# Scan layer of a four-layer network: state rows of 400 columns instead of 385, states starting at the seventeenth column

## The chip, the cores and the metric

The kernel runs on one core of a Trainium2 chip. Its time is the device time of one execution in microseconds (us). The core has five engines that run side by side and wait for each other on semaphores: TensorE (PE, with its weight loads as PEld), VectorE (DVE), ScalarE (ACT), GpSimd (POOL) and SyncE (SP), which here issues most of the DMAs. On-chip memory (SBUF) has 128 partitions; every engine works on all partitions at once and walks along the bytes of each. Matmuls write to a second memory, PSUM.

## The reference

An image batch x of 3 x 256 x 48 x 48 goes through four layers, each added to its own input after a group normalisation: an attention block (layer 0), a convolution whose 3x3 kernels are mixed from eight experts for each image (layer 1), a plain 3x3 convolution (layer 2), and a state-space scan (layer 3). The change touches layer 3 alone. Cut to what matters there, with b the image, t one of 2304 pixels in order, d one of 512 channels and n one of 16 states:

```python
dt = softplus(dt_raw @ dt_proj_w.T + dt_proj_b)          # (b, t, d)
def step(hst, inp):                                      # hst: (b, d, n)
    dt_t, B_t, C_t, u_t = inp
    dA = exp(dt_t[:, :, None] * A)
    hst = hst * dA + dt_t[:, :, None] * B_t[:, None, :] * u_t[:, :, None]
    y_t = einsum('bdn,bn->bd', hst, C_t)
    return hst, y_t
y = (ys + u * D) * silu(z)
out = y @ out_proj_w.T
```

So every channel and state is a recurrence h(t) = dA(t) h(t-1) + dtu(t) B(t) along the pixels, and the output sums h(t) C(t) over the 16 states. All data are float32.

## The kernel before, in words

Layers 0 to 2 fill the first 2025 us of the span. They use none of the tiles of the change.

In layer 3 the pixels of an image are cut into six chunks of CH = 384, so there are 18 chunks. A chunk's scan is 8 steps: four groups m of 128 channels, and two halves h of the 16 states. That makes 144 steps in the list `steps` (L1696). A step has one state tile `hs`: 128 partitions by 8 rows (two groups g by four q). A row is 385 float32: the state before the chunk in column 0, and one state for each of the 384 pixels behind it. A row of 385 floats is 1540 bytes, 24 times 64 and 4 more. There are three buffers for `hs`, two for `hc`, `dtr` and `dtur`, all in one pool (L1662).

A step goes through these stations:

- `first_states` (L1720): ACT copies eight starting states into column 0 (L1724), from a zero tile in the first chunk of an image, else from the states that the chunk before left.
- `fill` (L1705): the term dtu * B is written into columns 1 to 384. DVE writes the four rows with q = 0 and 1 from PSUM (L1711), POOL the four with q = 2 and 3 from the tile `dtur` (L1715).
- `decay` (L1732): ACT takes exp(dt * A) of one row into one of three PSUM slots `ps_da` (L1740). Column 0 of a slot holds 0.
- `scan` (L1745): DVE runs the recurrence over all 385 columns of one row, in place (L1748). The first column is multiplied by 0 and gets the first state added, so it passes the state on. Eight scans a step; the first four take the rows that DVE has filled, the last four those of POOL.
- `last_states` (L1726): ACT keeps the last column of the eight rows for the next chunk (L1730).
- `times_c` (L1752): POOL multiplies the eight rows by C into the tile `hc` (L1765). The very last step does this on DVE in two halves (L1759).
- `add_states` (L1770): PE folds `hc` into the sum `ps_y` (L1782), which starts with u * D (L1777), and `gate` (L1787) multiplies by silu(z) on DVE (L1789).

The order is written out by hand in the loop from L1800, and `keep_order` ties PE, DVE, ACT and POOL to it. In one step DVE issues eight scans and then the fill of the next step; POOL issues the fill of the next step and then `times_c` of this one; three decays run ahead of the scans. Between the scans the loop places the preparation of later chunks (`plan`, L1373): normalisation, projections, softplus (DVE at L1326 and L1327), and silu on ACT with two table loads (L1278, L228). A POOL fill may start when `times_c` has let go of the buffer that it writes; `times_c` of a step waits for that step's last scan; a scan of the second half waits for POOL's fill.

Of the kernel before, what the change touches and what calls it, by code (L numbers as in the profile page):

```python
# [9 lines left out]
F32 = mybir.dt.float32  # L10
I32 = mybir.dt.int32
AF = mybir.ActivationFunctionType
ALU = mybir.AluOpType
# [3 lines left out]
P = 128  # L17
# [8 lines left out]
CH = 384  # L26
# [10 lines left out]
DS = 16  # L37
DTR = 16
DCONV = 4


SUM_MIN, SUM_MAX = 1e-18, 1e18
# [41 lines left out]
def net(  # L84
# [21 lines left out]
    nc = tc.nc  # L106
# [1005 lines left out]
    def divide(block, *parts):  # L1112

        at = 0
        for name, rows, shape in parts:
            n = int(np.prod(shape))
            v = block[:rows, at : at + n]
            at += n
            if len(shape) > 1:
                names = "abc"[: len(shape)]  # L1120
                v = v.rearrange(
                    f"p ({' '.join(names)}) -> p {' '.join(names)}", **dict(zip(names, shape))
                )
            yield name, v

    def w3_rooms():
# [3 lines left out]
        w3v.update(divide(  # L1130
            block, ("w3sb", P, (NW3,)), ("wtap", P, (DCONV, CT, DI * P)), ("dtsb", DTR + 1, (DI * P,)),
            ("amat", P, (DI * DS,)), ("rep", P, (4, 32)), ("less", P, (2, P)), ("zero", P, (8,)),
            ("xn0", P, (CT, CH + DCONV - 1)), ("xn1", P, (CT, CH + DCONV - 1)),
        ))
# [23 lines left out]
    def x2_rooms():  # L1158
# [3 lines left out]
        winx, cwb = (t for _, t in divide(  # L1162
            block, ("winx", P, (CT, DI * P)), ("cwb", P, (DCONV, DI * P))
        ))
        nc.sync.dma_start(winx, w3x.rearrange("(t p) n -> p t n", p=P))
        for k in range(DCONV):
            nc.sync.dma_start(cwb[:, k, :], convw[k : k + 1, :].broadcast_to([P, DI * P]))
# [80 lines left out]
    def tokens(k):  # L1248

        xn = k.xn = room(k, "xn")  # L1250
        if k.c == 0:
            nc.gpsimd.memset(xn[:, :, : DCONV - 1], 0.0)
        else:
            nc.scalar.copy(xn[:, :, : DCONV - 1], k.before.xn[:, :, CH:])
        for ct in range(CT):
# [247 lines left out]
    with ExitStack() as l1:  # L1503
# [117 lines left out]
        for n, (k, h) in enumerate(halves):  # L1621
            layer, b = units[k]
# [33 lines left out]
    with ExitStack() as l3:  # L1656
# [5 lines left out]
        scn = l3.enter_context(tc.tile_pool(name="scn", bufs=2, reuse_waits="tile"))  # L1662
# [34 lines left out]
        tiles = {}  # L1697
# [7 lines left out]
        def fill(s):  # L1705

            at, m, h = steps[s]
            k = chunks[at]
            hs = tiles[s]
            bb = k.bc[0][:, 2 * h : 2 * h + 2, :].unsqueeze(2).broadcast_to([P, 2, 2, CH])  # L1710
            nc.vector.tensor_tensor(  # L1711
                hs[:, :, 0:2, 1:],
                k.ps[:, :, :CH].unsqueeze(1).broadcast_to([P, 2, 2, CH]), bb, ALU.mult,
            )
            nc.gpsimd.tensor_tensor(  # L1715
                hs[:, :, 2:4, 1:],
                k.rows[m][1].unsqueeze(1).broadcast_to([P, 2, 2, CH]), bb, ALU.mult,
            )

        def first_states(s):  # L1720
            at, m, h = steps[s]
            src = zero if chunks[at].c == 0 else state[m, h]
            hs = tiles[s] = scn.tile([P, 2, 4, CH + 1], F32, name="hs", bufs=3)
            nc.scalar.copy(hs[:, :, :, 0], src.rearrange("p (g q) -> p g q", g=2))  # L1724

        def last_states(s):  # L1726
            at, m, h = steps[s]
            if chunks[at].c < NCH - 1:
                t = state[m, h] = wp.tile([P, 8], F32, name=f"hst{m}{h}")
                nc.scalar.copy(t.rearrange("p (g q) -> p g q", g=2), tiles[s][:, :, :, CH])  # L1730

        def decay(n):  # L1732

# [10 lines left out]

        def scan(s, part):  # L1745
            g, q = parts_of_step[part]
            b = tiles[s][:, g, q, :]
            nc.vector.tensor_tensor_scan(  # L1748
                b, slots[(8 * s + part) % 3][:, : CH + 1], b, 0.0, ALU.mult, ALU.add
            )  # L1750

        def times_c(s):  # L1752
            at, m, h = steps[s]
            cb = chunks[at].bc[1][:, 2 * h : 2 * h + 2, :].unsqueeze(2)
            hc = scn.tile([P, 2, 4, CH], F32, name="hc")
            if s == len(steps) - 1:

                for g in range(2):
                    nc.vector.tensor_tensor(  # L1759
                        hc[:, g], tiles[s][:, g, :, 1:],  # L1760
                        cb[:, g].broadcast_to([P, 4, CH]), ALU.mult,
                    )
                tiles[s] = hc
                return
            nc.gpsimd.tensor_tensor(  # L1765
                hc, tiles[s][:, :, :, 1:], cb.broadcast_to([P, 2, 4, CH]), ALU.mult
            )
            tiles[s] = hc

# [24 lines left out]
        k.rows = {0: spread(k, 0)}  # L1794
        spread_pe(k, 0)
        first_states(0)
        fill(0)
        for n in range(3):
            decay(n)
        for s, (at, m, h) in enumerate(steps):  # L1800
            if m == 0 and h == 1 and at + 2 <= last:
                fetch(at + 2)
            for part in range(8):
                j = 4 * m + 2 * h + part // 4
                scan(s, part)
                decay(8 * s + part + 3)
                if part == 0 and h == 0:
                    c, n = (at, m + 1) if m + 1 < DI else (at + 1, 0)
                    if c <= last:
                        rows = getattr(chunks[c], "rows", {})  # L1810
                        chunks[c].rows = {**rows, n: spread(chunks[c], n)}
                if part == 4 and s + 1 < len(steps):
                    first_states(s + 1)
                if part % 4 == 1:
                    run(at, j, MID)
                if part % 4 == 2:
                    run(at, j, DONE)
                if h == 1 and part == 7 and s >= 3:
                    gate(*steps[s - 3][:2])
                if part % 4 == 3:  # L1820
                    run(at, j, LATE)
                if part == 3:
                    run(at, j, PE_)
            if s + 1 < len(steps):
                fill(s + 1)
            last_states(s)
            times_c(s)
            run(at, 4 * m + 2 * h + 1, PE_)
            if s >= 1:
# [129 lines left out]
```

## Time and profile before

| what | number |
|---|---|
| time, median of 3 runs | 3457.79 us (3455.21 to 3458.74) |
| the profiled execution's own time | 3459.61 us |
| its span, first to last instruction | 3458.2 us |
| DVE busy over the span | 2940.7 us (85%) |
| POOL busy over the span | 1430.7 us (41%) |
| ACT busy over the span | 2351.8 us (68%) |
| PE busy over the span | 3125.3 us (90%) |
| granted TensorE clock, mean | 0.944 |
| first scan to last scan | 2027.6 to 3436.0 us |

Busy shares are means over layers with different limits. A line of the profile gives line number, engine and operation, what is written from what (with partitions and elements), how often, the busy time together and the mean of one, and after the bar the idle time of the engine before it with what ended it.

### The profile page before, as it was taken

The numbers are of one execution on the slowest core, as the hardware profiler recorded it, in microseconds if no ns is written. First come the engines' busy times: TensorE is split into PE (matmuls) and PEld (weight loads), VectorE is DVE, ScalarE is ACT, GpSimd is POOL, SyncE is SP. The second block draws the span as 40 slices with busy tenths as digits, with TensorE's granted clock in tenths as the row PEclk, the third lists the DMA queues.
The fourth block names the chain that finished last, engine by engine and source line by source line (L and its number), as shares of the span: only waits on it lengthen the run. The fifth ranks groups of instructions, "written<-read, shape, count | busy, mean of one in ns | idle before, by whom it ended". The sixth has DMA issues, their size and how long they took to land.

```text
span 3458.2 us, 51943 instructions
## 1 busy us (share of the span) xinstructions
PE 3125.3 (90%) x20170; PEld 1499.8 (43%) x20170; DVE 2940.7 (85%) x3234; ACT 2351.8 (68%) x3508; POOL 1430.7 (41%) x385
## 2 busy tenths in 40 slices
PE   7999999999999999879999988888888888888885
PEld 4334343443433335447777743333343443333331
DVE  4799899859899994579965379999999999999998
ACT  3788888748888884422224457777777777777774
POOL 0000000000000001110000059999999999999997
PEclk9999999999999999989999989889999999988987
DMA  4000000010000003746402134445444444444441
GB/s 178 14 8 10 8 10 8 8 42 6 10 6 8 10 8 112 249 170 224 139 21 68 46 97 109 115 100 118 116 105 110 106 107 114 116 117 106 117 111 43
DMA packets 167603, 273.95 MB, mean 79 GB/s; under 512 B 30049, under 2 KB 134561, under 8 KB 165426
## 3 DMA queue, kind: packets, MB, share of 16 engines
q1 hardware_dynamic: 154114, 250.48, 26.9%
q10 hardware_dynamic: 13232, 20.06, 1.8%
q8 instruction: 160, 2.62, 0.3%
q14 instruction: 97, 0.79, 0.1%
HBM read 223.12 MB, written 47.10 MB: 78 GB/s over the span
## 4 chain that ended last, share of the span: by engine, by line
PE 54%; DVE 32%; ACT 8%; DMA 3%; issue 2%; POOL 0%; SPq 0%; DVEq 0%; ACTq 0%; POOLq 0%
DVE hs L1748 21%; PE ps_s L637 16%; PE acc L650 14%; PE ps_c L1513 8%; DVE hs L1711 4%; PE ps_g L1222 2%; PE ps_s L1030 2%; ACT ps_da L1740 2%; PE ps_y L461 2%; PE ps_m L664 1%; DVE u L295 1%; PE ps_m L710 1%; ACT L1278 1%; ACT L228 1%; PE acc L528 1%
## 5 line engine op out<-in xcount | busy, mean ns | idle before, releaser
L1748 DVE TENSOR_TENSOR_SCAN hs<-ps_da,hs 128x385 f32<-128x385 f32 x1152 | 1005.6, 938 | 54.4 <-ACT ps_da L1740 35.6
L641 ACT ACTIVATE pt<-ps_s 128x1024 f32<-128x1024 f32 x972 | 942.4, 1022 | 154.8 <-PE ps_s L637 142.2
L856 DVE TENSOR_TENSOR part<-part,pt 128x2048 f32<-128x2048 f32 x396 | 906.6, 2289 | 41.3 <-ACT pt L641 18.5
L1740 ACT ACTIVATE ps_da<-dtr,u 128x384 f32<-128x384 f32 x1152 | 656.0, 582 | 271.3 <-DVE hs L1748 248.4
L163 POOL TENSOR_TENSOR rstd<-ve,mhalf 128x2 f32<-128x2 f32 (+1 forms) x26 | 16.3, 629 | 1477.0 <-DVE ve L161 1477.0
L637 PE MATMUL ps_s<-q,kt 32*128 32x512 f32 (+1 forms) x4320 | 576.4, 592 | 0.1
L650 PE MATMUL acc<-pt,vt 128*32 128x512 f32 (+1 forms) x4320 | 520.9, 561 | 0.2
L1765 POOL TENSOR_TENSOR hc<-hs,x 128x3072 f32<-128x3072 f32 x72 | 446.3, 6198 | 19.8 <-DVE hs L1748 16.5
L1513 PE MATMUL ps_c<-vt,u 128*128 128x288 f32 x1728 | 433.9, 412 | 21.0 <-DVE u L262 21.0
L1765 POOL TENSOR_TENSOR hc<-hs,bc 128x3072 f32<-128x3072 f32 x71 | 438.8, 6181 | 18.6 <-DVE hs L1748 17.2
L1264 PE MATMUL ps_g<-u 128*128 128x384 f32 x1152 | 387.7, 491 | 8.2 <-ACT sz L1349 3.5
L1513 PEld LDWEIGHTS ps_c<-vt,u 128*128 128x128 f32 x1728 | 331.8, 193 | 117.8 <-issue 19.3
L1264 PEld LDWEIGHTS ps_g<-u 128*128 128x128 f32 x1152 | 214.4, 190 | 180.6 <-ACT ps_da L1740 18.7
L637 PEld LDWEIGHTS ps_s<-q,kt 32*128 32x128 f32 x4320 | 195.3, 183 | 199.1 <-issue 120.2
L1782 PE MATMUL ps_y<-hc,u 128*32 128x384 f32 x2304 | 244.8, 548 | 13.8 <-POOL hc L1765 13.8
L1715 POOL TENSOR_TENSOR hs<-dtur,x 128x1536 f32<-128x1536 f32 x72 | 248.4, 3450 | 6.9 <-DMA dtur<-dtud 6.9
L1715 POOL TENSOR_TENSOR hs<-dtur,bc 128x1536 f32<-128x1536 f32 x72 | 249.5, 3465 | 0.0
L650 PEld LDWEIGHTS acc<-pt,vt 128*32 128x32 f32 x4320 | 94.4, 108 | 353.4 <-issue 326.7
L1310 PE MATMUL ps_g<-wconv,u 17*128 17x384 f32 x144 | 79.2, 684 | 82.8 <-ACT x L1331 82.8
L1782 PEld LDWEIGHTS ps_y<-hc,u 128*32 128x32 f32 x2304 | 64.4, 117 | 172.4 <-issue 151.6
L321 POOL MEMSET xpad<- 128x212 f32 x12 | 5.6, 468 | 313.0 <-ACT xpad L1564 234.5
L1529 ACT COPY cb<-ps_c 128x288 f32<-128x288 f32 x48 | 19.2, 400 | 162.9 <-PE ps_c L1513 145.1
(246 smaller groups left out, 3685.3 us busy)
## 6 DMA issues: line engine op xcount, KB each, us to landing
wconv<-in_we SPq DMA_DIRECT2D x144, 384.0 KB, 4.3
dtr<-dtd SPq DMA_DIRECT2D x288, 192.0 KB, 3.9
dtur<-dtud SPq DMA_DIRECT2D x288, 96.0 KB, 4.2
wconv<-xd SPq DMA_DIRECT2D x36, 384.0 KB, 4.3
x<-bcd SPq DMA_DIRECT2D x72, 192.0 KB, 5.7
dtd<-x SPq DMA_DIRECT2D x36, 384.0 KB, 2.9
bc<-bcd SPq DMA_DIRECT2D x72, 192.0 KB, 6.1
yc<-ycat ACTq DMA_DIRECT2D x18, 576.0 KB, 5.0
```

The costliest lines, as they stand in the source:

```text
L637: nc.tensor.matmul(s[:, j, cols], kt[r, mt * P : (mt + 1) * P], q[r, :n], start=True, stop=True,)
L641: nc.scalar.activation(p[:, h0 : h0 + 2, :], s, AF.Exp)
L650: nc.tensor.matmul(acc[h * HD : (h + 1) * HD, :n], vt[:, mt, g * P + h * HD : g * P + (h + 1) * HD], p[:, h, cols], start=mt == 0, stop=mt ...
L856: ): nc.vector.tensor_tensor(part, first, p, ALU.add)
L1264: nc.tensor.matmul(bank[m % 2], w3v["wtap"][:, tap, ct, m * P : (m + 1) * P], k.xn[:, ct, tap : tap + CH], start=tap == 0 and ct == 0, sto ...
L1513: nc.tensor.matmul(pc[:, :HN], u[:, i, dy, ct, m * P : (m + 1) * P], vt[:, i, ct, dy * TW : dy * TW + HN], start=ct == 0 and dy == 0, stop ...
L1711: nc.vector.tensor_tensor(hs[:, :, 0:2, 1:], k.ps[:, :, :CH].unsqueeze(1).broadcast_to([P, 2, 2, CH]), bb, ALU.mult,)
L1715: nc.gpsimd.tensor_tensor(hs[:, :, 2:4, 1:], k.rows[m][1].unsqueeze(1).broadcast_to([P, 2, 2, CH]), bb, ALU.mult,)
L1740: nc.scalar.activation(slots[n % 3][:, 1 : CH + 1], chunks[at].rows[m][0][:, q, :], AF.Exp, scale=amat[:, col : col + 1],)
L1748: nc.vector.tensor_tensor_scan(b, slots[(8 * s + part) % 3][:, : CH + 1], b, 0.0, ALU.mult, ALU.add)
L1765: nc.gpsimd.tensor_tensor(hc, tiles[s][:, :, :, 1:], cb.broadcast_to([P, 2, 4, CH]), ALU.mult)
L1782: nc.tensor.matmul(k.y_ps[32 * q : 32 * q + 32, :CH], fold, hc[:, g, q, :], start=False, stop=h == 1 and g == 1,)
```

## The change

The rows of `hs` become ROW + CH = 400 columns long, 1600 bytes or 25 times 64. The first state moves from column 0 to column 15, and the 384 states from columns 1 to 384 to columns 16 to 399. A scan runs over columns 15 to 399, again 385 of them. Everything that reads or writes the tile is moved along. Sizes, counts and engines of the instructions stay.

```diff
+ROW = 16
...
             nc.vector.tensor_tensor(
-                hs[:, :, 0:2, 1:],
+                hs[:, :, 0:2, ROW:],
                 k.ps[:, :, :CH].unsqueeze(1).broadcast_to([P, 2, 2, CH]), bb, ALU.mult,
             )
             nc.gpsimd.tensor_tensor(
-                hs[:, :, 2:4, 1:],
+                hs[:, :, 2:4, ROW:],
...
-            hs = tiles[s] = scn.tile([P, 2, 4, CH + 1], F32, name="hs", bufs=3)
-            nc.scalar.copy(hs[:, :, :, 0], src.rearrange("p (g q) -> p g q", g=2))
+            hs = tiles[s] = scn.tile([P, 2, 4, ROW + CH], F32, name="hs", bufs=3)
+            nc.scalar.copy(hs[:, :, :, ROW - 1], src.rearrange("p (g q) -> p g q", g=2))
...
-                nc.scalar.copy(t.rearrange("p (g q) -> p g q", g=2), tiles[s][:, :, :, CH])
+                nc.scalar.copy(t.rearrange("p (g q) -> p g q", g=2), tiles[s][:, :, :, ROW + CH - 1])
...
-            b = tiles[s][:, g, q, :]
+            b = tiles[s][:, g, q, ROW - 1 :]
...
-                        hc[:, g], tiles[s][:, g, :, 1:],
+                        hc[:, g], tiles[s][:, g, :, ROW:],
...
-                hc, tiles[s][:, :, :, 1:], cb.broadcast_to([P, 2, 4, CH]), ALU.mult
+                hc, tiles[s][:, :, :, ROW:], cb.broadcast_to([P, 2, 4, CH]), ALU.mult
```

## The prediction

> **What bounds the kernel now.** The change touches only the scan layer, so I read first the busy time of each engine over that stretch (2025 to 3441 us; columns: length, then busy us and instructions of PE, PEld, DVE, ACT, POOL, then clock and DMA).
>
> ```profile
> core 0: us, PE busy (x) PEld busy (x) DVE busy (x) ACT busy (x) POOL busy (x), PEclk, DMA share, GB/s
> 2025.00:3441.00 1416.00, 1164.49 (x4876) 530.07 (x4874) 1358.98 (x1521) 1082.74 (x2070) 1368.86 (x289) 0.89 0.45 108
> ```
>
> DVE is busy for 1359 of 1416 us and POOL for 1369: both 96 to 97%. The page's share of POOL over the whole span (41%) hides that. Next, who waited for whom in that stretch: first DVE's and ACT's waits, then POOL's.
>
> ```profile
> ACT ps_da L1740 <- DVE hs L1748: 248.4, 399, 4.1
> ```
> ```profile
> DVE hs L1748 <- ACT ps_da L1740: 35.6, 53, 1.5
> DVE hs L1748 <- POOL hs L1715: 3.8, 1, 3.8
> ```
> ```profile
> POOL hc L1765 <- DVE hs L1748: 33.8, 31, 1.6
> POOL hs L1715 <- DMA dtur<-dtud: 6.9, 1, 6.9
> POOL hc L1765 <- PE ps_g L1222: 2.6, 2, 1.4
> POOL hc L1765 <- DVE x L1789: 1.8, 1, 1.8
> ```
>
> DVE waited for POOL once, 3.8 us, at the first step. POOL waited for DVE 31 times, ACT 399 times. So **DVE sets the pace**, and POOL is the next bound, close behind: it has 33.8 + 2.6 + 1.8 = 38.2 us of idle time in 144 steps, 0.265 us a step. The page's chain agrees: DVE 32% of the span, POOL 0%. Third, the groups that touch the tile `hs`, on the page:
>
> ```profile
> L1748 DVE TENSOR_TENSOR_SCAN hs<-ps_da,hs 128x385 f32<-128x385 f32 x1152 | 1005.6, 938 | 54.4 <-ACT ps_da L1740 35.6
> ...
> L1765 POOL TENSOR_TENSOR hc<-hs,x 128x3072 f32<-128x3072 f32 x72 | 446.3, 6198 | 19.8 <-DVE hs L1748 16.5
> ...
> L1765 POOL TENSOR_TENSOR hc<-hs,bc 128x3072 f32<-128x3072 f32 x71 | 438.8, 6181 | 18.6 <-DVE hs L1748 17.2
> ...
> L1715 POOL TENSOR_TENSOR hs<-dtur,x 128x1536 f32<-128x1536 f32 x72 | 248.4, 3450 | 6.9 <-DMA dtur<-dtud 6.9
> L1715 POOL TENSOR_TENSOR hs<-dtur,bc 128x1536 f32<-128x1536 f32 x72 | 249.5, 3465 | 0.0
> ```
>
> A step costs POOL 6.19 + 3.46 = 9.65 us. DVE's steps take 9.0 us in the middle of a chunk and 10.9 where the preparation at L1326 and L1327 falls (starts of first scans, from the timeline); the mean is 9.81. POOL falls behind in the short steps and catches up in the long ones.
>
> **The change part by part.** No instruction is added, removed or moved. The built program of the changed kernel has the same instructions in the same order with the same waits on PE, DVE, ACT, POOL and SP, DMA issues included. Element counts stay: 385 a scan, 1536 a fill, 3072 a `times_c`. So all that can change is the **duration of the accesses to `hs`**, and of those to `hc`, which lies behind `hs` in its pool: the built program puts the three `hs` buffers at 0, 32 and 0 bytes past a multiple of 64 before, and `hc` at 32; after, all of them at 0.
>
> *Scans, 1152 on DVE, on the path.* In the old tile row r starts 1540 r bytes in, which is 4r past a multiple of 64. Eight rows by two kinds of buffer give sixteen different starts, so the old trace already holds the experiment. Durations (min, median, max) of the scans, and three successive steps, which use three different buffers:
>
> ```profile
> L1748 DVE TENSOR_TENSOR_SCAN hs<-ps_da,hs x1152: 931/934/964, 2027.6 to 3436.0; 128x385 f32<-128x385 f32 x192
> ```
> ```profile
> 3394.09 6.91 DVE L1748 TENSOR_TENSOR_SCAN hs<-ps_da,hs 128x385 f32<-128x385 f32 x8
> ...
> 3403.21 6.91 DVE L1748 TENSOR_TENSOR_SCAN hs<-ps_da,hs 128x385 f32<-128x385 f32 x8
> ...
> 3411.88 6.91 DVE L1748 TENSOR_TENSOR_SCAN hs<-ps_da,hs 128x385 f32<-128x385 f32 x8
> ```
>
> Eight scans take 6.91 us whatever the buffer. Sorted scan by scan, row 0 takes 960.3 ns in a buffer at 0 and 960.1 ns in the one at 32 (the first scan of a step is the long one); row 7 of the buffer at 32 starts 60 bytes past a multiple, which is where column 15 of the new rows puts every scan, and takes 933.3 ns, against 932.6 in a buffer at 0. Starts follow each other every 850 ns in all rows. I take **0** for the scans. The ends: every scan at the lowest duration, 931, instead of the mean 938, would give 1152 x 7 ns = 8 us; every scan 0.7 ns longer (933.3 for 932.6) costs 0.8 us.
>
> *DVE's fills, 144, on the path.* By buffer they take 1740.4, 1740.2 and 1740.3 ns. I take 0; the spread of the row over a chunk's two kinds of step (1732 to 1748) bounds it at 144 x 8 ns = 1.2 us either way.
>
> *POOL's fills and `times_c`.* By `hs` buffer: 3457.5, 3457.0, 3458.4 and 6188.9, 6190.1, 6189.8 ns. No buffer shows anything, but in each at least seven of eight rows are off a multiple of 64, so a tile with all rows on one is not in the trace. The nearest rows are those above: every second chunk keeps B and C in a block called x, 32 bytes past a multiple of 64, the others in bc, at 0, and their own rows of 384 columns stay there. The aligned operand makes `times_c` 17 ns shorter and the fill 15 ns longer. I take 0 for the pair, within 32 ns a step. **Faster bound**: if POOL took no time at all, DVE would save its one wait, 3.8 us; nothing else on the path waits for POOL but the tail, where PE's last sums start at 3439.0 us, when L1777 ends, 0.3 us behind POOL's end at 3438.7. So POOL alone can't bring more than about 4 us. **Slower bound, near**: the slowest `times_c` and fill (6273 and 3523) against the medians (6197 and 3448) are 0.15 us a step, under the 0.265 of idle time, so hidden but for the last chunk, where no preparation lets POOL catch up: some ten steps x 0.15 = 1.5 us. **Slower bound, far**: the last step's products run on DVE beside POOL, and the first of them is held up:
>
> ```profile
> 3432.50 6.18 POOL L1765 TENSOR_TENSOR hc<-hs,bc 128x3072 f32<-128x3072 f32 x1
> ...
> 3437.29 4.67 DVE L1759 TENSOR_TENSOR hc<-hs,bc 128x1536 f32<-128x1536 f32 x2
> ```
>
> The two took 3.00 and 1.75 us: 1.26 us lost. Both POOL instructions of each step losing that would cost (2.51 - 0.265) x 144 = 323 us. My value lies by the near rows.
>
> *ACT's copies* (L1724 and L1730, 264 of 192 ns, steps of 400 columns instead of 385): all lie between 185 and 207 ns; 15 ns x 264 = 4 us on an engine that waits 248 us for DVE. If that cover were gone it would be those 4 us. *PE's reads of `hc`* keep their shape; median 486 ns; PE is in the chain only in the tail, with 16 such matmuls, so 0.
>
> Sum: 0 for DVE, at most 32 ns x 10 = 0.3 us in the tail from POOL. From the profiled execution that is 3459.6 us (span 3458.2 and 1.4 around it); that one lies 1.8 above the median, so against the median the forecast is **3457.8 us**, no change.
>
> *The Trainium skill against the change.* The page GPSIMD Engine Reference, section 3.1, gives two-input `tensor_tensor` about 2.5 cycles an element because both inputs share one read port, and 4497 ns for 2048 elements; addresses are no term in it. At that rate, 2.196 ns, `times_c` would be 6.75 us (an estimate from that page), and this trace has 6.19: there is no stall on top of the rate that alignment could take away, and by the page the sum is 0 too. The page SBUF — State Buffer, section "Who interferes with whom", knows one contention only, the lock on the port pair of VectorE and GpSimd. By it the first rival below costs nothing.
>
> **The rivals.**
> 1. *Slower: POOL becomes the bound.* With every row, `hs` buffer and `hc` on multiples of 64, accesses of POOL's two inputs and output, or of POOL and DVE, may fall together. It decides from 0.265 us a step on (2.7% of 9.65). A fifth of what L1759 lost on each of the two instructions is 0.50 us: (0.50 - 0.265) x 144 = 34 us, 3492. For it: POOL's 97%, and that the aligned fill is the longer one. Against it: 15 ns is all that the rows show.
> 2. *Faster: the scans get shorter.* 931 ns for all gives 8 us, 3450; it needs 6 ns a scan to pass 0.2%. Against it: sixteen starts without a difference.
> 3. *The change does only half of what it says.* Scans start at 60 past a multiple of 64, and B and C of every second chunk stay at 32. If alignment matters to POOL but only with all operands aligned, half the chunks gain. The time is then bounded as above: 3454 to 3458.
>
> **How the numbers follow.** Nothing changes: 0.70. Rival 3: 0.10. Rival 1: 0.12. Rival 2: 0.08. A measurement of this kernel tells about 0.2%, 7 us, from no change. The first two lie within it (0.80), rival 1 is slower (0.12), rival 2 faster (0.08). The range takes in the 8 us of rival 2 with 1 for spread, 3449, and on the other side a POOL pair 0.35 us longer, (0.35 - 0.265) x 144 = 12 us, 3470; what rival 1 gives beyond that is left out.
>
> **What would show it.** Right: scans at 934 median and 850 ns apart, 1740 for DVE's fills, POOL's pair within 32 ns of 9.65 us, POOL still waiting some 30 times for DVE. Wrong: a POOL pair above 9.92 us with DVE waiting for L1715 in many steps (rival 1), scans 6 ns shorter (rival 2), or `times_c` shorter only in the bc chunks (rival 3).

## The result and the profile after

The changed kernel takes 3498.44 us (median of 4 runs, 3495.99 to 3504.02) against 3458.26 (4 runs, 3455.21 to 3460.85): ratio 1.0119, 95% interval 1.0101 to 1.0136. It is slower by 40 us; the forecast was no change and a range that ended at 3470.

The groups that touch `hs`, on the page after (one line further down in the code):

```profile
L1749 DVE TENSOR_TENSOR_SCAN hs<-ps_da,hs 128x385 f32<-128x385 f32 x1152 | 1011.8, 940 | 85.3 <-POOL hs L1716 36.4
...
L1766 POOL TENSOR_TENSOR hc<-hs,x 128x3072 f32<-128x3072 f32 x72 | 482.9, 6707 | 0.3 <-POOL hs L1716 0.3
L1766 POOL TENSOR_TENSOR hc<-hs,bc 128x3072 f32<-128x3072 f32 x71 | 476.3, 6708 | 0.0
...
L1716 POOL TENSOR_TENSOR hs<-dtur,x 128x1536 f32<-128x1536 f32 x72 | 248.4, 3451 | 6.7 <-DMA dtur<-dtud 6.7
L1716 POOL TENSOR_TENSOR hs<-dtur,bc 128x1536 f32<-128x1536 f32 x72 | 248.9, 3456 | 0.0
```

One number moved: `times_c` takes 6.71 us instead of 6.19, in all steps. The fills and the scans are as before. The waits over the scan stage, of DVE and then of POOL:

```profile
DVE hs L1749 <- POOL hs L1716: 36.4, 56, 3.8
DVE hs L1749 <- ACT ps_da L1741: 33.5, 52, 1.5
```
```profile
POOL hs L1716 <- DMA dtur<-dtud: 6.7, 1, 6.7
POOL hc L1766 <- POOL hs L1716: 0.3, 1, 0.3
```

The two engines have changed places. POOL no longer waits for DVE at all (31 times before); DVE waits for POOL's fills 56 times. From the first scan to the last, the stage is 1447.2 us long instead of 1408.4: +38.7. The tail behind the last scan is 22.8 us instead of 22.2. The rest of the difference between these two profiled executions, 5 us, lies ahead of the scans (the first one starts at 2032.5 instead of 2027.6 us), in layers that the change does not touch; the times of the changed kernel spread by 8 us.

Why should the product of `hs` and C get 8% longer when rows are aligned, and the fill, which writes the same rows, not? Four theories went into the first runs: **A**, the product is slow where both inputs' rows start at the same place in some small block of bytes; **B**, reading rows that start on a multiple of 64 is slow by itself; **C**, the place of the output `hc` matters (it moved from 32 past a multiple of 64 to 0); **D**, the row pitch of 1600 bytes does.

### The profile page after: what moved, and what is told of

Read it like the earlier page. It is cut to its first block, busy times and chain, and to the rows that moved or that the text cites. A ratio compares the mean times of both kernels' runs of the same rounds, so it can differ in the third digit from the quotient of the medians.

```text
span 3502.4 us, 51943 instructions
## 1 busy us (share of the span) xinstructions
PE 3160.0 (90%) x20170; PEld 1507.4 (43%) x20170; DVE 2948.5 (84%) x3234; ACT 2358.6 (67%) x3508; POOL 1509.0 (43%) x385
## 5 line engine op out<-in xcount | busy, mean ns | idle before, releaser
L1766 POOL TENSOR_TENSOR hc<-hs,x 128x3072 f32<-128x3072 f32 x72 | 482.9, 6707 | 0.3 <-POOL hs L1716 0.3
L1766 POOL TENSOR_TENSOR hc<-hs,bc 128x3072 f32<-128x3072 f32 x71 | 476.3, 6708 | 0.0
L1783 PE MATMUL ps_y<-hc,u 128*32 128x384 f32 x2304 | 262.2, 581 | 76.9 <-POOL hc L1766 75.9
L1223 PE MATMUL ps_g<-wconv,u 128*128 128x384 f32 x144 | 81.7, 736 | 48.3 <-ACT x L1332 48.3
```

The lines of the kernel that those rows point to most:

```text
L1223: nc.tensor.matmul(bank[to], w3v["less"][:, int(to != ct), :], k.xg[:, ct, :], start=ct == 0, stop=ct == CT - 1,)
L1766: nc.gpsimd.tensor_tensor(hc, tiles[s][:, :, :, ROW:], cb.broadcast_to([P, 2, 4, CH]), ALU.mult)
L1783: nc.tensor.matmul(k.y_ps[32 * q : 32 * q + 32, :CH], fold, hc[:, g, q, :], start=False, stop=h == 1 and g == 1,)
```

## The experiments

The kernel before was timed beside them on the same chip: 3455.3 us (one run) beside the two kernels with `hc` moved and the two sweeps, 3456.35 (median of 13 runs) beside the four that follow (states at column 14), 3456.04 (10 runs) beside the last two. A time with a ratio is a median of several runs; the others are one run each, and what is read from those is the durations of POOL's instructions, 143 or 144 of a kind in a trace and eight or more at each place of a sweep.

**The place of hc.** In both kernels the same edit, which moves `hc` by 32 bytes:

```diff
+            if s == 0:
+                scn.tile([P, 8], F32, name="gap", bufs=1)
             hc = scn.tile([P, 2, 4, CH], F32, name="hc")
```

> The kernel before with 32 unused bytes ahead of hc, so that hc starts at a multiple of 64 bytes as it does after the change; hs keeps its rows of 385. Theory A (the product times_c is slow where both inputs' rows start at the same place within some block of bytes), theory B (reading hs rows that all start on a multiple of 64 is slow by itself) and theory D (the row pitch of 1600 bytes is what is slow) all expect no change: times_c 6.19 us, about 3458 us. Theory C (where the output hc starts, alone or against hs, is what is slow) expects times_c between 6.4 and 6.7 us and 3475 to 3498 us.

Measured: 3458.1 us, `times_c` 6.18 us:

```profile
L1767 POOL TENSOR_TENSOR hc<-hs,x 128x3072 f32<-128x3072 f32 x72 | 444.6, 6175 | 21.4 <-DVE hs L1748 19.4
...
L1767 POOL TENSOR_TENSOR hc<-hs,bc 128x3072 f32<-128x3072 f32 x71 | 438.7, 6179 | 18.1 <-DVE hs L1748 16.7
```

> The changed kernel with 32 unused bytes ahead of hc, so that hc starts 32 bytes past a multiple of 64 as it did before the change. Theories A, B and D expect the changed kernel's numbers: times_c 6.71 us, about 3498 us. Theory C expects times_c back at 6.19 us and about 3458 us.

Measured: 3495.6 us. Here the records mislead at first sight: `times_c` reads 6.85 us and the fills 3.63, longer than in the changed kernel. But each record overlaps the next one by 0.19 us; from start to start the two instructions follow each other after 3.44 and 6.66 us, as in the changed kernel (3.42 and 6.68). Three in a row (start, length):

```profile
2600.20 6.93 POOL L1768 TENSOR_TENSOR hc<-hs,bc 128x3072 f32<-128x3072 f32 x1
2606.88 3.69 POOL L1716 TENSOR_TENSOR hs<-dtur,bc 128x1536 f32<-128x1536 f32 x1
2610.33 6.92 POOL L1768 TENSOR_TENSOR hc<-hs,bc 128x3072 f32<-128x3072 f32 x1
```

C falls, by both runs, for the two places that it was about.

**A sweep of the start of the states**, in the changed kernel (both fills and the last states are moved along in the same way):

```diff
+        def lead(s):
+            return 1 + 2 * (s % 8) + s // 16 % 2
...
-            nc.scalar.copy(hs[:, :, :, ROW - 1], ...
+            nc.scalar.copy(hs[:, :, :, lead(s) - 1], ...
...
-            b = tiles[s][:, g, q, ROW - 1 :]
+            b = tiles[s][:, g, q, lead(s) - 1 : lead(s) + CH]
...
-                hc, tiles[s][:, :, :, ROW:], cb.broadcast_to([P, 2, 4, CH]), ALU.mult
+                hc, tiles[s][:, :, :, lead(s) : lead(s) + CH], cb.broadcast_to([P, 2, 4, CH]), ALU.mult
```

> The changed kernel's rows of 400 columns, but the states of a step start at column 1 + 2 (s mod 8) + (s // 16 mod 2), so that over the steps they start at each of the sixteen places within 64 bytes, and all eight rows of one step at the same one; pitch 1600 bytes and hc at 0 throughout. Theory A: times_c 6.71 us only where the start agrees with that of the other input (0 in the bc chunks, 32 in the x chunks), 6.19 us elsewhere, mean about 6.22, about 3459 us. Theory B: 6.71 us only in steps that start at 0, 6.19 elsewhere, mean about 6.22, 3459 us. Theory D: 6.71 us in all steps, 3498 us. If blocks shorter than 64 bytes count (16 or 32), the curve shows a period of that length. POOL's fills, which write these rows, are expected at 3.45 us in all places by every theory but C, DVE's scans at 934 ns.

Measured: 3451.6 us. POOL's timeline in a chunk with C at 32 (start, length; the fills between are left out), with states that start 4, 12, 20 and 28 bytes past a multiple of 64:

```profile
2661.80 6.73 POOL L1769 TENSOR_TENSOR hc<-hs,x 128x3072 f32<-128x3072 f32 x1
...
2671.89 5.64 POOL L1769 TENSOR_TENSOR hc<-hs,x 128x3072 f32<-128x3072 f32 x1
...
2680.89 6.72 POOL L1769 TENSOR_TENSOR hc<-hs,x 128x3072 f32<-128x3072 f32 x1
...
2690.97 5.65 POOL L1769 TENSOR_TENSOR hc<-hs,x 128x3072 f32<-128x3072 f32 x1
```

The curve has two levels and a period of 16 bytes. By the start modulo 16, averaged over all steps: 0: 6.73, 4: 6.71, 8: 5.64, 12: 5.64 us, the same in x and bc chunks. The fills that write these rows take 3.43 to 3.47 us on average at each of the sixteen places, without that pattern. D falls, since the pitch is 1600 throughout; so does B, since 4, 16, 20 and 32 are as slow as 0. The first half of a 16-byte block is slow, the second fast: that is A with a block far shorter than the 64 bytes that I had in mind, or a rule about `hs` alone. The level of 6.19 us that every theory expected off the slow places does not occur: the fast one is 5.64.

**A sweep of the other inputs**, in the changed kernel (`k.at` is the number of the chunk; the tile behind bc1 is made 16 floats longer):

```diff
-            dtur = scn.tile([P, 2, CH], F32, name="dtur")
+            off = (4 * k.at + m) % 16
+            dtur = scn.tile([P, 2 * CH + 16], F32, name="dtur")[:, off : off + 2 * CH]
+            dtur = dtur.rearrange("p (a n) -> p a n", a=2)
...
             t = room(k, f"bc{j}")
+            if j == 1 and k.at % 2:
+                off = 2 * (k.at // 2) % 16
+                t = t[:, off : off + 4 * CH].rearrange("p (a n) -> p a n", a=4)
```

> The changed kernel's hs and hc, but the other inputs of POOL are moved: dtur, first input of the fills, starts 0, 4, ... 60 bytes past a multiple of 64 by turns, and in the bc chunks (every second one) the tile with C, second input of times_c, starts at 0, 8, ... 56 by turns; the x chunks keep C at 32. Theory A: times_c in the bc chunks falls from 6.71 to 6.19 us wherever C does not start at the same place as hs, and stays at 6.71 in the x chunks only if 32 counts as the same place as 0; the fills, whose two inputs start at the same place in both kernels, get shorter where dtur is moved, to about 3.2 us (an estimate: with times_c slow at 6.71 for 3072 elements and the fill at 3.45 for 1536, the slow rate is 2.12 ns an element and 0.2 us is fixed; at the fast rate, (6.19 - 0.2) / 3072 = 1.95 ns, a fill is 3.19 us). Theory B: times_c stays at 6.71 us throughout, the fills get shorter as in A. Theories C and D: nothing moves, 6.71 and 3.45 us. Time: 3498 us where nothing moves, down to 3458 where the pair falls under 9.92 us.

Measured: 3458.0 us. The last `times_c` of a bc chunk with C at 24, then x, with dtur at 4 and then at 8, and the first of the next bc chunk with C at 32:

```profile
2655.55 5.64 POOL L1772 TENSOR_TENSOR hc<-hs,bc 128x3072 f32<-128x3072 f32 x1 [1.65 <-DVE hs L1755]
...
2681.50 3.46 POOL L1722 TENSOR_TENSOR hs<-dtur,x 128x1536 f32<-128x1536 f32 x1
2684.91 6.76 POOL L1772 TENSOR_TENSOR hc<-hs,x 128x3072 f32<-128x3072 f32 x1
2691.60 2.93 POOL L1722 TENSOR_TENSOR hs<-dtur,x 128x1536 f32<-128x1536 f32 x1
...
2744.00 6.78 POOL L1772 TENSOR_TENSOR hc<-hs,bc 128x3072 f32<-128x3072 f32 x1
```

With `hs` left at 0, moving C alone by 8, 24, 40 or 56 bytes brings 5.63 to 5.68 us; 16, 32 and 48 leave 6.76. The fills take 2.91 to 2.96 us with dtur at 8 or 12 modulo 16, and 3.44 to 3.50 at 0 or 4. So either input can do it, and the fills of the kernel before were at the slow rate all along. The 3.2 us that I expected of a fast fill is the mean of a kernel with half its fills fast (3.20 measured), not the fast level.

**Is it the two inputs' relation, or each one's place?** Both moved by 8 bytes, in the bc chunks only (`ROW = 14` in rows of 400, and C's tile two floats wider and read from its third):

```diff
-ROW = 16
+ROW = 14
...
+        t = wp.tile([P, 4 * CH + 4], F32, name="bc1")
+        rooms["bc1"].append(t[:, 2 : 2 + 4 * CH].rearrange("p (a n) -> p a n", a=4))
```

> The changed kernel's rows of 400 columns, but the states start at column 14, 56 bytes past a multiple of 64 (8 past a multiple of 16) in all rows; and in the bc chunks C is moved by 8 bytes as well, while the x chunks keep it at a multiple of 16. Theory A, as the sweeps narrowed it (POOL's two-input product is slow where both inputs lie in the same half of their 16 bytes, whatever that half is): times_c 6.71 us in the bc chunks, 5.64 us in the x chunks. Rival (it is slow only where an input lies in the first half of its 16 bytes): 5.64 us in both, or 5.64 in bc and 6.71 in x. By A the pair of POOL is 9.63 us a step on average, so the time is near that of before, 3456 us.

Measured: 3460.4 us. POOL's groups:

```profile
L1768 POOL TENSOR_TENSOR hc<-hs,bc 128x3072 f32<-128x3072 f32 x71 | 477.0, 6718 | 1.1
L1768 POOL TENSOR_TENSOR hc<-hs,x 128x3072 f32<-128x3072 f32 x72 | 406.0, 5639 | 40.9 <-DVE hs L1751 31.8 <-PE ps_g L1223 4.4 <-DVE x L1792 2.4
```

Both in the second half is as slow as both in the first: it is the relation. A stands, with a block of 16 bytes and two halves of 8.

One thing about the relation stays open. The second input (C, or B in the fills) always started at 0 or 8 past a multiple of 16; against 0 the first was tried at 0, 4, 8 and 12, against 8 at 0 and 8. "Slow where both start in the same half" fits all of these, and so does "slow where the first starts 0 or 4 bytes behind the second, modulo 16". The two rules part only where the second input starts at 4 or 12, and no run has that; for the kernels here they say the same.

**What POOL's speed is worth.** First the changed kernel with `ROW = 14` alone, then with dtur two floats on as well:

> The changed kernel with one thing other: the states start at column 14 instead of 16, so 8 bytes past a multiple of 16 in all rows, while B, C and dtur stay at multiples of 16. Theory A: times_c 5.64 us in all steps, fills 3.45, the pair 9.09 us, so POOL waits for DVE for some 100 us; since DVE sets the pace, the time comes back to that of before and no further than the 4 us that POOL could bring: 3453 to 3458 us, ratio 0.999 to 1.0. Rival (POOL's speed was on the path in the kernel before too, because both engines were 97% busy): the 0.53 us that times_c is shorter than before show in part, 3400 to 3440 us.

Measured: 3456.22 us, ratio 0.9998 (0.9988 to 1.0007). `times_c` 5.64 us, fills 3.45. POOL's longest wait, and DVE's waits for ACT and POOL:

```profile
POOL hc L1766 <- DVE hs L1749: 91.7, 65, 2.2
```
```profile
DVE hs L1749 <- ACT ps_da L1741: 33.8, 52, 1.3
...
DVE hs L1749 <- POOL hs L1716: 3.8, 1, 3.8
```

> As r2, and dtur is moved by 8 bytes, so that the fills' two inputs lie in different halves too. Theory A: fills 2.93 us, times_c 5.64, the pair 8.57 us; time as r2, 3452 to 3458 us, because DVE is the bound and its scans stay 850 ns apart. The rival of r2 expects a further fall.

Measured: 3456.5 us, one run; fills 2.90, `times_c` 5.64, stage from first to last scan 1408.6 us:

```profile
L1767 POOL TENSOR_TENSOR hc<-hs,bc 128x3072 f32<-128x3072 f32 x71 | 400.1, 5636 | 88.1 <-DVE hs L1750 63.6
...
L1717 POOL TENSOR_TENSOR hs<-dtur,bc 128x1536 f32<-128x1536 f32 x72 | 209.3, 2906 | 0.1
```

POOL is 1.1 us a step faster than in the kernel before, and nothing comes of it: it waits for DVE.

**Using the room.** As the last one, and one of DVE's products goes to POOL:

```diff
             nc.vector.scalar_tensor_tensor(pdt, pdt, 0.0, k.dt[:, m, :], ALU.max, ALU.add)
-            nc.vector.tensor_tensor(k.dtu[:, m, :], pdt, k.u[:, m, :], ALU.mult)
...
             nc.scalar.copy(k.dt[:, m0 + j, :], bank[j])
+        two = slice(m0, m0 + 2)
+        nc.gpsimd.tensor_tensor(k.dtu[:, two, :], k.dt[:, two, :], k.u[:, two, :], ALU.mult)
```

> As r3, and the product dt * u (L1327 of before, 72 instructions of 0.56 us on DVE) goes to POOL, which takes it from the copy of dt that ACT makes, 36 instructions of two rows. If DVE is the bound and POOL has been given room, DVE's 72 x 0.56 = 40 us come off: about 3415 to 3425 us, ratio 0.988 to 0.991; POOL's load is 8.57 + 36 x 1.7 / 144 = 9.0 us a step, under DVE's 9.5. Rival (the steps with preparation wait for ACT and PE anyway, so the time that DVE gives up turns into waits of DVE for ACT): 3435 to 3455 us.

Measured: 3414.43 us (4 runs), ratio 0.988 (0.986 to 0.990), the fastest version here, below both kernels. The stage is 1365.6 us, 43 less than before, where 40 us of DVE's work was taken away. DVE's waits stay what they were, and the new product costs POOL 1.8 us for each pair of rows:

```profile
DVE hs L1751 <- ACT ps_da L1743: 34.1, 51, 1.5
...
DVE hs L1751 <- POOL hs L1718: 3.2, 1, 3.2
```
```profile
L1333 POOL TENSOR_TENSOR dtu<-x,u 128x768 f32<-128x768 f32 x18 | 32.5, 1805 | 9.4 <-ACT x L1331 5.4 <-DMA bc<-bcd 4.0
```

The same move in the kernel before, with nothing shifted in memory:

> The kernel before (rows of 385) with the product dt * u moved from DVE to POOL, and nothing moved in memory. If what counts is POOL's total against DVE's: POOL has 9.65 + 36 x 1.80 / 144 = 10.10 us a step, and DVE has 0.28 less than before; POOL is the bound, and the time is near that of the changed kernel (10.16 us a step), 3485 to 3495 us, although DVE does less. Rival (the gain came from the shorter DVE work, whatever POOL's speed): 3415 to 3430 us.

Measured: 3477.28 us, ratio 1.0061 (1.0039 to 1.0084). The direction is as expected and the size is not. I had reckoned 10.10 us a step from the records of other kernels, against 10.16 in the changed kernel, a difference of 9 us over 144 steps. The records of this run add up to less: two of the 36 products lie ahead of the first fill, and `times_c` and the fills read 6.16 and 3.43 us, not 6.19 and 3.46. Their sum is 1436 us where the changed kernel's is 1456, and the stage is 19 us shorter than there. Consecutive records overlap, here by some 0.03 us; counted once, POOL is busy for 1426 us, and the stage is 1427.9 us long. Behind its first fill POOL rests for 1.4 us in all, and DVE waits for it 66 times:

```profile
DVE hs L1749 <- POOL hs L1716: 69.2, 66, 3.6
DVE hs L1749 <- ACT ps_da L1741: 23.7, 39, 1.6
```

So the gain of the version above is neither the product's move nor the faster POOL alone: it takes both.

**The sum or the long instruction?** The changed kernel with dtur two floats on, `times_c` left slow:

> The changed kernel, with dtur alone moved by 8 bytes: times_c stays slow at 6.71 us, the fills fall from 3.45 to 2.91. If it is the sum of POOL's two instructions that decides (9.62 us a step, under DVE's pace of 9.8), the time comes back to 3453 to 3460 us, with the slow times_c in place. Rival (the long times_c itself holds up what waits for it, the buffers of hs and PE's sums): 3480 to 3500 us.

Measured: 3455.34 us, ratio 1.0002 (0.9989 to 1.0015), with `times_c` at 6.74 and fills at 2.91 us. POOL waits for DVE again, DVE for POOL only once, and the long product holds nothing up:

```profile
L1767 POOL TENSOR_TENSOR hc<-hs,bc 128x3072 f32<-128x3072 f32 x71 | 478.8, 6743 | 16.2 <-DVE hs L1750 15.3
...
L1717 POOL TENSOR_TENSOR hs<-dtur,bc 128x1536 f32<-128x1536 f32 x72 | 210.2, 2919 | 0.0
```
```profile
POOL hc L1767 <- DVE hs L1750: 32.1, 31, 1.6
```
```profile
DVE hs L1750 <- POOL hs L1717: 3.2, 1, 3.2
```

## Why the prediction was wrong

- **The step that failed**: "I take 0 for the pair, within 32 ns a step". It is 0.51 us a step, all of it in `times_c` (6.19 to 6.71). The rows that I leaned on could not show it. C at 0 or at 32 past a multiple of 64 is the same half of 16 bytes. And the old rows of 1540 bytes, 96 times 16 and 4 more, start at 4, 8, 12 and 0 past a multiple of 16 in turn: in every buffer, four of eight rows share C's half and four don't. So each old `times_c` had half its rows at the slow places of the sweep and half at the fast ones, and its length is the mean of the two levels: (6.71 + 5.64) / 2 = 6.18. Comparing buffers compared equal mixtures. I had noted that a tile with all rows alike is not in the trace, and still took the nearest rows' value.
- **The bound and the decision point were right.** Rival 1 was priced at 0.50 us a step as 34 us; with the measured 0.51 the same sum, (0.51 - 0.265) x 144, is 35 us, and the stage grew by 38.7. That the price came so near is luck: 0.50 was a fifth, freely chosen, of what a product on DVE had lost beside POOL, and the runs show no link between the two. POOL's two inputs were among the places that the rival named ("accesses of POOL's two inputs and output, or of POOL and DVE, may fall together"), for multiples of 64 and with a chance of 0.12; the block turned out to be 16 bytes, and no run shows a part of the output's place. The range's upper end stopped at a pair 0.35 us longer.
- **The scans, DVE's fills and ACT's copies**: right. Scans have a median of 934 ns as before; DVE's fills take 1740 ns on average as before, the copies 185 to 207.
- **"POOL alone can't bring more than about 4 us"**: right. POOL 0.55 and 1.1 us a step faster left the time where it was.
- **Rival 3, that alignment matters only with all operands aligned**: wrong in its reason. The x chunks, with C at 32, are as slow as the bc chunks.
- **The Trainium skill**: the page GPSIMD Engine Reference, section 3.1, has no term for addresses, and I read its rate as showing that there was no stall to remove. That reading was wrong: the states at column 14 took 0.55 us off `times_c`. (The 2.5 cycles an element that I gave for section 3.1 stand in the page's section 2.1; 3.1 has about 2.6. The price in nanoseconds did not use them.) This case has two rates. In the slow relation 1536 and 3072 elements take 3.45 and 6.71 us, some 2.12 ns an element and 0.2 us fixed, and the moved product of 768, 1.80 us, lies by the same line; in the fast one 1536 and 3072 take 2.90 and 5.64 us, 1.78 ns and 0.17 us. The page's 4497 ns for 2048 lies by the slow line, which gives 4.54 us (an estimate from these rows). And the rule of SBUF — State Buffer, "Who interferes with whom", that only the port pair of VectorE and GpSimd contends, says nothing of the places of one instruction's own two inputs; here these make it 19% longer (6.71 against 5.64 us).
- **Open**: why the place within 16 bytes counts. The runs show which relation is slow, not what in the chip makes it so. Other element types, and products with one input, were not tried.

## What to carry to other kernels

"Aligned" is not by itself fast: ask which inputs the alignment gives the same start, and sweep the start over one block of bytes inside one kernel, by step, before fixing it. Where an instruction runs over rows whose starts differ, its length is a mean, and equal means over buffers say nothing about the single cases. Two engines at 96 and 97% were here one bound and one cover: speed in the second was worth nothing until work was moved to it, and a loss in it cost once it was over the cover of 0.265 us a step.

## What the runs showed of the hardware that I had not expected

- GpSimd's two-input float32 product takes 1.78 ns an element where the rows of its inputs start in different halves of a 16-byte block, and 2.12 ns where they start in the same half, in the combinations that were tried. The output's place made no difference where it was moved (fills of 3.43 to 3.47 us at sixteen places; `times_c` the same with `hc` moved by 32 bytes).
- VectorE's scans, of which one input lies in PSUM, showed nothing of the kind: 932 to 940 ns on average at each of the sixteen places (the first scan of a step left out).
- Records of consecutive GpSimd instructions overlap, by 0.03 to 0.07 us on average in most runs and by 0.19 in one; start to start is the measure.
